# Softmax row sums in a transformer block: one running sum of four key tiles instead of a tree of pairs, with the diagonal's first tile in the last of them

## The chip, the core and the metric

The kernel runs on one core of a Trainium2 chip. The metric is the device time of one execution in microseconds (us). Before the change the median of three runs is 2449.43 us, with 2448.74 the lowest and 2451.66 the highest.

## The reference

One block of a conditioned transformer, all in float32: x is [2, 2048, 512], 16 heads of 32 dimensions, a hidden layer of 2048. The part that matters here is causal attention.

```
mod = silu(condition) @ Wada + bada            # six vectors per batch row
xm = layernorm(x) * (1 + sc_a) + sh_a
q, k, v = split(xm @ Wqkv)
scores = where(causal, q @ k.T * scale, -inf)
attn = softmax(scores);  out = attn @ v
x = x + gt_a * (out @ Wproj + bproj)
x = x + gt_m * (gelu(modulated layernorm(x) @ W1 + b1) @ W2 + b2)
```

The kernel never divides inside the attention loop. It computes the exponentials E of the scores less their row maximum, the product of E with v, and the row sums of E, and multiplies by the inverse sums afterwards.

## The kernel before

The program goes in stages: q, k, v of batch row 0; attention of row 0 (about 229 to 760 us in the profile); projection of row 0 and q, k, v of row 1; attention of row 1 (about 1085 to 1577 us); projection and the two layers of the hidden network. The change lies in the two attention stages, in `attention_phase`.

**Units and steps.** A stage has 16 units. A unit is a pair (c, i): c counts four groups of four heads (HC = 4), i counts four blocks of 512 queries (QB = 512). For c = 0 the blocks come in the order 0, 1, 2, 3, for the other groups in the order 0, 2, 1, 3. Unit 5, say, has i = 2, unit 14 has i = 1, and the last, unit 15, has i = 3. A unit goes through the key tiles of 128 keys (TQ = 4 to a query block) in steps. The 4i tiles ahead of the diagonal block take one step each. I write T for step 4i: it has the diagonal's first tile, with all 512 queries. Step T+1 has two narrower tiles (384 and 128 queries) side by side, and T+2 the last (256 queries).

**One step.** `scores_t` makes PSUM tiles `st`, one for each head: first a matmul of `fold` and `sel` that puts in minus the row maximum, then the product of keys and queries. The ScalarE (ACT) takes the exponentials, L576, into SBUF tiles `e`. On the diagonal steps the GpSimd (POOL) sets what lies above the diagonal to zero with an affine select, L582. Between these products PE also makes the scores `s` of coming units, whose row maxima the VectorE (DVE) reduces at L446 and L451; now and then such a score borrows a bank of `st`. The number per step comes from a plan of costs (`due`, `count`), in which the row sums don't appear. PE's matmuls are all issued at L199, and every engine works through its own list in the order in which it was written.

**Delayed work.** What uses the exponentials is put into a list, `pending`, with the number of the step at whose end it may be issued; `flush` issues what is due after the products of a step. The value products (`values`, tile `o`) of a step are issued two steps later (LAG = 2), so those of step T at the flush of T+2, those of T+1 at the flush of T+3, which is the first step of the next unit, and those of T+2 at the flush of T+4.

**Row sums.** They are matmuls with a block of ones (tile `sm`), a set of four for the four heads, the heads side by side on the PE array as for the value products. Ahead of the diagonal one set serves four tiles: POOL first adds tiles 0 and 1 (`pair_sums`, `ee<-e`), then 2 and 3, and then the two pairs in place (`four_sums`, `ee<-ee`), four adds each time, one for each head. The third addition is issued one step late (`later`); at the end of a unit it is split in two halves, one at step T after the selects of T, one at T+1 after those of T+1. Each diagonal step has sets of its own, issued with its value products. In the last unit of a stage the adds are DVE's (`add`, L604). Tiles `e` rotate through 12 buffers, tiles `ee` through 12.

Of the kernel before, what the change touches and what calls it, by code (L numbers as in the profile page):

```python
# [27 lines left out]
def dit_block_kernel(  # L28
# [32 lines left out]

    nc = tc.nc
    B, T, D = x.shape
    HID = W1.shape[1]
# [3 lines left out]
    HC = P // HD  # L70
    TQ = QB // P
# [1 line left out]
    MTT = MT // P  # L73
    NG = T // MT
    LAG = 2
    E_BUFS = 12
    EE_BUFS = 12
    AHEAD = 3

    const = ctx.enter_context(tc.tile_pool(name="const", bufs=1))  # L80
# [33 lines left out]
    for n in range(2):  # L114

        f = bp.tile([P, QB + P], F32R, tag=f"fold{n}", name=f"fold{n}")
# [84 lines left out]
    def act(ins):  # L201

        return tc.keep_in_program_order(ins)
# [322 lines left out]
    def attention_phase(row):  # L526
        b, vv, kst, qst = row.b, row.vv, row.kst, row.qst
        with pool(f"att{b}") as ap, pool(
# [6 lines left out]
            def scores_t(u, step, n):  # L535
# [29 lines left out]
                for h in range(HC):  # L565
                    at = 0
                    for j, q in tiles:
# [6 lines left out]
                        at += QB - q  # L574
                    e = ap.tile([P, QB], F32, tag="e", name="e", bufs=E_BUFS)
                    act(nc.scalar.activation(e[:, :w], sts[h][:, :w], AF.Exp))  # L576
# [19 lines left out]
            def new_sums():  # L596
                return [
                    ap.tile([P, QB], F32, tag="ee", name="ee", bufs=EE_BUFS)
                    for _ in range(HC)
                ]  # L600

            def add(u, h, dst, x, y):
                engine = nc.vector if u == len(units) - 1 else nc.gpsimd
                act(engine.tensor_tensor(dst, x, y, ALU.add))  # L604

            def pair_sums(u, es0, es1):
                out = new_sums()
                for h in range(HC):
                    add(u, h, out[h], es0[h], es1[h])
                return out  # L610

            def four_sums(u, ee0, ee1, heads):
                for h in heads:
                    add(u, h, ee0[h], ee0[h], ee1[h])

            def products(dst, lhs, es, q0, at, first, last):
                for h in range(HC):
                    mm(
                        dst[h * HD : (h + 1) * HD, q0:], lhs(h),
                        es[h][:, at : at + QB - q0], start=first, stop=last,  # L620
                    )

            def finish(u, o, sm):

                c, i = units[u]
                ot = ap.tile([P, QB], F32, tag="ot", name="ot", bufs=2)
                act(nc.scalar.copy(ot, o))
                sums = ap.tile([P, QB], F32, tag="sums", name="sums", bufs=2)
                act(nc.scalar.copy(sums, sm))
                nc.sync.dma_start(sums_d[b][u], sums[0:P:HD, :])  # L630
                nc.sync.dma_start(od[b][i][:, c, :], ot)


            pending = []
            now = 0

            def flush(upto):
                while pending and pending[0][0] <= upto:
                    pending.pop(0)[1]()
# [16 lines left out]
            def due(u, step):  # L656

                rate, past = 0.0, weight[step]
                for v in range(u + 1, len(units)):

                    left = sum(weight[step : max(step + 1, starts[v] - 3)])
                    rate = max(rate, (cum[v] - row.spent) / left)
                return row.spent + rate * past

            for u, (c, i) in enumerate(units):
                if NQ <= u + AHEAD < len(units):
                    row.load_queries(u + AHEAD)
                if u % NQ == 0 and c + 1 < C:
                    row.load_keys(c + 1, 0, NG)
                steps = len(steps_of[u])  # L670
                for n_step, tiles in enumerate(steps_of[u]):
                    last = n_step == steps - 1
                    if n_step == 0:
                        summed, later = set(), []
                        o = ps_op.tile([P, QB], F32, tag="o", name="o")
                        sm = ps_op.tile([P, QB], F32, tag="sm", name="sm")
                    ready = row.at

                    n = row.count(
                        due(u, starts[u] + n_step) - QB // 2, u + AHEAD - (n_step < 2)  # L680
                    )
                    es, rest = scores_t(u, n_step, n)
                    rest = len(row.todo) - rest
                    make_rows = False
                    if u + 1 < len(units) and row.rows_made == u + 1:
                        if last:
                            row.score(row.count(cum[-1], u + 1))
                        make_rows = last or (ready > u + 1 and n_step >= 1)
                    row.inverses(u, n_step)
                    if u == len(units) - 1:  # L690
                        row.prepare(n_step)
                    flush(now)
                    if make_rows:
                        row.rows(u + 1)
                    row.score(max(0, len(row.todo) - rest))

                    def tile_by_tile(dst, lhs, es, tiles, first, last):
                        at = 0
                        for n, (j, q) in enumerate(tiles):
                            products(  # L700
                                dst, lambda h: lhs(j, h), es, q, at,
                                first and n == 0, last and n == len(tiles) - 1,
                            )
                            at += QB - q

                    def values(es=es, tiles=tiles, c=c, o=o, first=n_step == 0, last=last):
                        tile_by_tile(
                            o,
                            lambda j, h: vv[:, j, (c * HC + h) * HD : (c * HC + h + 1) * HD],
                            es, tiles, first, last,  # L710
                        )

                    def row_sums(es, last, tiles=((0, 0),), sm=sm, summed=summed):
                        first = not summed
                        summed.add(len(summed))
                        tile_by_tile(sm, lambda j, h: ones[:, :HD], es, tiles, first, last)

                    if later:
                        four_sums(u, *later.pop(0))

                    pending.append((now + LAG, values))
                    if n_step >= i * TQ:
                        pending.append(
                            (
                                now + LAG,
                                lambda f=row_sums, es=es, tiles=tiles, last=last: f(
                                    es, last, tiles
                                ),
                            )
                        )  # L730
                    elif n_step % 2 == 0:
                        even = es
                    else:
                        ee = pair_sums(u, even, es)
                        if n_step % 4 == 1:
                            ee0 = ee
                        else:

                            end = n_step + 1 == i * TQ
                            for heads in ([(0, 1), (2, 3)] if end else [range(HC)]):  # L740
                                later.append((ee0, ee, heads))
                            pending.append(
                                (
                                    now + LAG + 2 + end,
                                    lambda f=row_sums, ee=ee0: f(ee, False),
                                )
                            )
                    if last:
                        pending.append((now + LAG, lambda u=u, o=o, sm=sm: finish(u, o, sm)))
                    pending.sort(key=lambda p: p[0])  # L750
                    now += 1
# [248 lines left out]
    with pool("wada") as wp, pool("qkv0") as qp, pool(  # L1000
# [110 lines left out]
        with pool("hl0") as hp:  # L1111
# [8 lines left out]
            quarters.store()  # L1120

    attention_phase(row)


    first, row = row, Row(1)
    with pool("qkv1") as qp, pool("ps_qkv1", bufs=6, space=PSUM) as ps_mm:
# [22 lines left out]
        with pool("hl1") as hp:  # L1149
# [5 lines left out]
            quarters.store()  # L1155

    attention_phase(row)
    ps_s_cm.__exit__(None, None, None)

# [4 lines left out]
    with ExitStack() as mlp:  # L1164
# [248 lines left out]
        for m in range(NM):  # L1413
            h = [
                [
                    mp.tile([P, 4, MT], F32, tag="h4", name="h4", bufs=2 * FC // 4)
                    for _ in range(FC // 4)
                ]
                for _ in range(2)
            ]  # L1420
# [87 lines left out]
```

## Time and profile before

| What | Value |
|---|---|
| median of the runs | 2449.43 us (2448.74 to 2451.66) |
| profiled execution, its own time | 2449.97 us |
| span of the profile | 2448.3 us |
| PE busy | 2409.8 us, 98% of the span |
| DVE busy | 1348.9 us, 55% |
| POOL busy | 986.8 us, 40% |
| ACT busy | 894.3 us, 37% |
| mean granted TensorE clock | 0.994 |

The span is from the first to the last instruction; the profiled execution's own time has 1.67 us around it. A busy share is an average over stages that differ, so it has to be read by stage. A group of instructions is given by its line, engine, operation and tiles (out<-in), its count, its busy time and the mean duration of one; matmuls overlap, so a matmul's price is read from the distance between starts. A matmul in float32 leaves two records. In the timeline a row has start, length, engine, line, operation and the number of merged instructions.

### The profile page before, as it was taken

How to read it: one execution, taken by the hardware profiler on the slowest of the kernel's cores; microseconds unless marked ns; L12 is line 12 of the kernel's file. 1: busy time of each engine (PE TensorE's matmuls, PEld its weight loads, DVE VectorE, ACT ScalarE, POOL GpSimd, SP SyncE). 2: the span in 40 equal slices, each digit the busy share in tenths (PEclk: the TensorE clock that was granted, in tenths of full speed). 3: DMA queues.
4: the chain of work that ended last, by engine and by line, in shares of the span. 5: the costliest groups of instructions: out<-in, count | busy, mean ns of one | idle time of the engine just before them, and what ended most of it. 6: DMA issues, size and time to landing. Idle time of an engine off the chain costs nothing. (4 is left out here: it accounts for less than half of the span.)

```text
span 2448.3 us, 31029 instructions
## 1 busy us (share of the span) xinstructions
PE 2409.8 (98%) x10989; PEld 1174.7 (48%) x10989; DVE 1348.9 (55%) x2828; ACT 894.3 (37%) x1668; POOL 986.8 (40%) x1167
## 2 busy tenths in 40 slices
PE   8999999999999999999999999999999999999998
PEld 3445555555554444555555555444444444444443
DVE  3455766666656636566666666673354263343424
ACT  2212555555554112255555555523213212312310
POOL 1051886776773460078677678312002101200200
PEclk9999999999999999999999999999999999999999
DMA  6667115151225795530515123362223223222322
GB/s 224 210 222 195 45 31 121 27 113 44 83 99 181 231 309 170 145 70 23 117 40 113 45 64 118 135 204 84 86 94 134 90 95 131 93 90 87 119 86 99
DMA packets 132853, 285.72 MB, mean 117 GB/s; under 512 B 13473, under 2 KB 42701, under 8 KB 127833
## 3 DMA queue, kind: packets, MB, share of 16 engines
q1 hardware_dynamic: 126224, 257.46, 35.4%
q0 software_dynamic: 6384, 26.25, 3.0%
q8 instruction: 86, 1.41, 0.2%
q14 instruction: 71, 0.57, 0.1%
q10 hardware_dynamic: 88, 0.02, 0.0%
HBM read 209.76 MB, written 81.79 MB: 119 GB/s over the span
## 5 line engine op out<-in xcount | busy, mean ns | idle before, releaser
L576 ACT ACTIVATE e<-st 128x512 f32<-128x512 f32 (+1 forms) x1152 | 574.1, 578 | 459.6 <-PE st L199 402.3
L451 DVE TENSOR_REDUCE mx<-s 128x1 f32<-128x512 f32 x606 | 408.7, 687 | 220.9 <-PE s L199 220.0
L604 POOL TENSOR_TENSOR ee<-e 128x512 f32<-128x512 f32 x336 | 421.1, 1298 | 210.1 <-ACT e L576 210.1
L199 PE MATMUL s<-kst,qst 128*128 128x512 f32 (+3 forms) x1032 | 465.3, 453 | 5.8 <-DVE mx L451 2.9
L199 PE MATMUL st<-qst,kst 128*128 128x512 f32 (+3 forms) x1280 | 411.3, 389 | 0.0
L446 DVE CUSTOM_DVE_ANT_0 junk<-s,causal 128x512 bf16<-128x512 f32 (+3 forms) x426 | 208.9, 490 | 156.3 <-PE s L199 148.3
L199 PE MATMUL o<-e,vv 128*32 128x512 f32 (+3 forms) x2560 | 293.6, 540 | 0.0
L1279 POOL TENSOR_TENSOR c<-c 128x512 f32<-128x512 f32 x32 | 40.8, 1275 | 625.6 <-DVE c L1241 606.0
L199 PE MATMUL ps_h<-sx,w 128*128 128x512 f32 x640 | 286.7, 592 | 0.0
L199 PE MATMUL ps_y<-sh,w 128*128 128x512 f32 x640 | 277.8, 594 | 0.0
L199 PEld LDWEIGHTS st<-qst,kst 128*128 128x128 f32 x1280 | 229.0, 189 | 94.5 <-issue 62.5
L199 PEld LDWEIGHTS s<-kst,qst 128*128 128x128 f32 x1032 | 195.0, 189 | 155.6 <-DVE mx L451 49.3
L199 PE MATMUL ps_qk<-xmT,wqkv 128*128 128x512 f32 x512 | 241.5, 600 | 2.2 <-DVE xmT L256 2.2
L582 POOL TENSOR_SCALAR_AFFINE_SELECT e<-e 128x128 f32<-128x128 f32 (+1 forms) x384 | 122.8, 353 | 268.7 <-ACT e L576 265.7
L1241 DVE TENSOR_TENSOR h<-c,ps_h 128x512 f32<-128x512 f32 x128 | 88.0, 687 | 232.5 <-PE ps_h L199 232.5
L604 POOL TENSOR_TENSOR ee<-ee 128x512 f32<-128x512 f32 x168 | 212.3, 1300 | 0.0
L199 PEld LDWEIGHTS ps_h<-sx,w 128*128 128x128 f32 x640 | 121.1, 190 | 150.2 <-issue 149.5
L199 PEld LDWEIGHTS ps_y<-sh,w 128*128 128x128 f32 x640 | 121.3, 191 | 148.5 <-issue 147.1
L1265 ACT ACTIVATE h<-h,cols 128x512 f32<-128x512 f32 x128 | 92.4, 722 | 181.6 <-DVE h L1241 181.6
L199 PE MATMUL st<-fold,sel 32*128 32x512 f32 (+1 forms) x1152 | 149.3, 482 | 2.1 <-DVE mhl L467 1.0
L199 PEld LDWEIGHTS ps_qk<-xmT,wqkv 128*128 128x128 f32 x512 | 94.9, 192 | 98.7 <-issue 92.6
L199 PEld LDWEIGHTS st<-fold,sel 32*128 32x128 f32 x1152 | 58.8, 182 | 147.6 <-ACT e L576 75.3
(128 smaller groups left out, 2359.0 us busy)
## 6 DMA issues: line engine op xcount, KB each, us to landing
qst<-q SPq DMA_DIRECT2D x128, 256.0 KB
w<-w1d SPq DMA_DIRECT2D x34, 896.0 KB
w<-w2d SPq DMA_DIRECT2D x28, 1024.0 KB
kst<-k SPq DMA_DIRECT2D x24, 1024.0 KB
q<-hl SPq DMA_DIRECT2D x32, 512.0 KB
k<-hl SPq DMA_DIRECT2D x32, 512.0 KB
kst<-k SPq DMA_DIRECT2D x32, 256.0 KB
w<-in_L_cond_W_dram POOLq DMA_DIRECT2D x64, 128.0 KB, 4.5
```

What stands on the lines that cost most here:

```text
L199: return tc.keep_in_program_order(nc.tensor.matmul(*args, **kw))
L446: nc.vector.tensor_tensor_reduce(junk[:, :w], s[:, :w], causal[:, QB - w :], 1.0, MASKED, ALU.add, ALU.max, m,)
L451: nc.vector.tensor_reduce(m, s[:, :w], axis=AX.X, op=ALU.max)
L576: act(nc.scalar.activation(e[:, :w], sts[h][:, :w], AF.Exp))
L582: nc.gpsimd.affine_select(d, d, pattern=[[0, len(tiles)], [1, P]], compare_op=ALU.is_ge, fill=0.0, base=0, channel_multiplier=-1,)
L604: act(engine.tensor_tensor(dst, x, y, ALU.add))
L1241: nc.vector.tensor_tensor(dst, x, y, op)
L1265: nc.scalar.activation(d, d, AF.Gelu, bias=col(r_b1 + chunk, 1))
L1279: nc.gpsimd.tensor_tensor(c1_, c1_, c2_, ALU.subtract)
```

## The change

`pair_sums`, `four_sums` and the list `later` go. In each group of four steps ahead of the diagonal, step 1 now begins a chain with the sum of tiles 0 and 1 (`begin_chain`), step 2 adds its tile to it and step 3 adds its own (`add_to`). The number of adds for four tiles stays at twelve. In units with i > 0 the last chain also takes the exponentials of step T, after that step's selects: four adds more, and no set of row sums for T alone. The chain that takes T is summed at the flush of T+4, and the sums of step T+1 move from the flush of T+3 to that of T+4, after the chain's. Units with i = 0 have no chain and keep their sums. There are 16 buffers for `e`, so four steps, and 8 for `ee`.

```
-    E_BUFS = 12
-    EE_BUFS = 12
+    E_BUFS = 16
+    EE_BUFS = 8
...
-            def pair_sums(u, es0, es1):
-                out = new_sums()
+            def add_to(u, chain, es):
                 for h in range(HC):
-                    add(u, h, out[h], es0[h], es1[h])
-                return out
-
-            def four_sums(u, ee0, ee1, heads):
-                for h in heads:
-                    add(u, h, ee0[h], ee0[h], ee1[h])
+                    add(u, h, chain[h], chain[h], es[h])
+
+            def begin_chain(u, es0, es1):
+                chain = new_sums()
+                for h in range(HC):
+                    add(u, h, chain[h], es0[h], es1[h])
+                return chain
...
-                    if later:
-                        four_sums(u, *later.pop(0))
-
                     pending.append((now + LAG, values))
-                    if n_step >= i * TQ:
+                    sums_of, wait = None, 0
+                    if n_step < i * TQ:
+                        k = n_step % TQ
+                        if k == 0:
+                            even = es
+                        elif k == 1:
+                            chain = begin_chain(u, even, es)
+                        else:
+                            add_to(u, chain, es)
+                        if k == TQ - 1 and n_step + 1 < i * TQ:
+                            sums_of, wait = (chain, False), 2
+                    elif i and n_step == i * TQ:
+                        add_to(u, chain, es)
+                        sums_of, wait = (chain, False), 2
+                    else:
+
+                        sums_of, wait = (es, last, tiles), i > 0 and not last
+                    if sums_of:
                         pending.append(
-                            (
-                                now + LAG,
-                                lambda f=row_sums, es=es, tiles=tiles, last=last: f(
-                                    es, last, tiles
-                                ),
-                            )
+                            (now + LAG + wait, lambda f=row_sums, s=sums_of: f(*s))
                         )
-                    elif n_step % 2 == 0:
-                        even = es
-                    else:
-                        ee = pair_sums(u, even, es)
-                        if n_step % 4 == 1:
-                            ee0 = ee
-                        else:
-
-                            end = n_step + 1 == i * TQ
-                            for heads in ([(0, 1), (2, 3)] if end else [range(HC)]):
-                                later.append((ee0, ee, heads))
-                            pending.append(
-                                (
-                                    now + LAG + 2 + end,
-                                    lambda f=row_sums, ee=ee0: f(ee, False),
-                                )
-                            )
```

More of the change, by code (lines that the diff above doesn't have):

```diff
@@ L673, in attention_phase @@
                     if n_step == 0:
-                        summed, later = set(), []
+                        summed = set()
                         o = ps_op.tile([P, QB], F32, tag="o", name="o")
```

## The prediction

> **What bounds the kernel now.** I read the page first, then the busy time by stage, the groups by form, and the timelines of PE, POOL and ACT around the ends of two units. The two attention stages are the only ones that the change touches.
>
> ```profile
> PE 2409.8 (98%) x10989; PEld 1174.7 (48%) x10989; DVE 1348.9 (55%) x2828; ACT 894.3 (37%) x1668; POOL 986.8 (40%) x1167
> ```
> ```profile
> 229.00:760.00 531.00, 528.81 (x3613) 271.74 (x3613) 351.68 (x845) 293.73 (x586) 367.16 (x428) 0.99 0.30 76
> ...
> 1100.00:1580.00 480.00, 478.16 (x3314) 243.42 (x3314) 316.16 (x759) 265.99 (x532) 333.19 (x394) 1.00 0.29 76
> ```
> ```profile
> L604 POOL TENSOR_TENSOR ee<-e 128x512 f32<-128x512 f32 x336 | 421.1, 1298 | 210.1 <-ACT e L576 210.1
> ...
> L604 POOL TENSOR_TENSOR ee<-ee 128x512 f32<-128x512 f32 x168 | 212.3, 1300 | 0.0
> ...
> L199 PE MATMUL sm<-ee,ones 128*32 128x512 f32 x384 | 51.1, 604 | 0.0
> ```
> In the second block the columns are the stretch, its length, and busy time of PE, PEld, DVE, ACT, POOL. PE is busy 528.8 of 531.0 us in the first attention stage and 478.2 of 480.0 in most of the second: whatever PE no longer does there is gained, as long as it still waits for nothing. POOL is the next fullest, 367 of 531 (69%), and it is far from evenly filled: it idles in the units of i = 0 and works without a gap at the ends of the others. The list of waits has PE and its weight loads waiting for POOL hardly at all (5.5 us in 17 pieces of at most 0.4), so today's margins hold. The question is whether they hold after the change.
>
> **What leaves PE.** The end of unit 5 (i = 2), PE's timeline:
>
> ```profile
> 415.49 1.07 PE L199 MATMUL o<-e,vv 128*32 128x512 f32 x8
> 416.49 0.49 PE L199 MATMUL s<-kst,qst 128*128 128x512 f32 x1
> ...
> 418.48 1.07 PE L199 MATMUL o<-e,vv 128*32 128x512 f32 x8
> 419.36 1.04 PE L199 MATMUL sm<-e,ones 128*32 128x512 f32 x8
> 420.33 0.50 PE L199 MATMUL st<-fold,sel 32*128 32x512 f32 x4
> ...
> 422.70 1.07 PE L199 MATMUL o<-e,vv 128*32 128x384 f32 x16
> ```
> A set of four value products alone takes 415.49 to 416.49, 1.00 us; followed by a set of row sums 418.48 to 420.33, 1.85. Four row sums so cost 0.85 us, start to start (the durations overlap and add up to more). The change drops the row sums of the first diagonal tile in every unit of i > 0: 12 units a batch row, 24 in all, 96 matmuls of two profile records each, which the instruction lists of the two builds confirm. 24 x 0.85 = **20.4 us off PE**. The sums of tiles T+1 and T+3 are only moved one flush later, into a run of the same kind of matmul: no set more or less, no new change between kinds, so I put this at nothing. Scores on PE, exponentials and DMA issues keep their order; at each stage's end two neighbouring stores swap, which costs nothing as the first load that needs them, r<-sum, follows both either way, and twice a stage a reduction of DVE (0.69 us) swaps with small neighbours, in stretches where PE waited for DVE under 0.5 us: nothing too.
>
> **What goes to POOL.** Outside the last unit of each row, 22 units get four adds more (88). In the trace eight adds stretch from 401.58 to the next start at 411.52: 1.24 us each, 4.97 for a set of four, 109 us in all. It lies beside PE, but in a worse place. Before, a group of four steps gave POOL four adds at its step 1, four at step 3, four at the next step 0 (split in two halves around the selects at a unit's end). Now steps 1, 2, 3 give four each, and step T four more. The adds of T stand in POOL's queue ahead of the selects of step T+1, and PE's value products wait for those selects. That is the new wait. Its neighbour, the chain's own sum, is not wanted before two flushes later.
>
> I walk POOL's queue for two units, with times of exponentials from ACT's timeline, 4.97 us for four adds and 1.01, 1.45 and 1.05 us for the selects of T, T+1, T+2 (from start-to-start).
>
> ```profile
> 401.58 10.01 POOL L604 TENSOR_TENSOR ee<-e 128x512 f32<-128x512 f32 x8
> 411.52 1.07 POOL L582 TENSOR_SCALAR_AFFINE_SELECT e<-e 128x128 f32<-128x128 f32 x4
> 412.55 2.55 POOL L604 TENSOR_TENSOR ee<-ee 128x512 f32<-128x512 f32 x2
> 415.03 1.50 POOL L582 TENSOR_SCALAR_AFFINE_SELECT e<-e 128x256 f32<-128x256 f32 x4
> ```
> ```profile
> 711.73 2.06 ACT L576 ACTIVATE e<-st 128x512 f32<-128x512 f32 x4 [0.18 <-PE st L199]
> 715.15 2.06 ACT L576 ACTIVATE e<-st 128x512 f32<-128x512 f32 x4 [1.36 <-PE st L199]
> 718.95 2.06 ACT L576 ACTIVATE e<-st 128x512 f32<-128x512 f32 x4 [1.73 <-PE st L199]
> 722.09 2.07 ACT L576 ACTIVATE e<-st 128x512 f32<-128x512 f32 x4 [1.08 <-PE st L199]
> ```
> ```profile
> 728.61 1.07 PE L199 MATMUL o<-e,vv 128*32 128x384 f32 x16
> ```
> Unit 5: the adds begin at 384.46 as they do now, and run in one piece: sets end at 389.4, 394.4, 399.4; second chain 404.4, 409.3, 414.3 (its last exponentials were ready at 407.5). Selects of T 415.3, adds of T 420.3, selects of T+1 421.7, of T+2 422.8. PE wants T at 418.48 (3.2 us to spare) and T+1 at 422.70 less the 0.85 saved, 421.85: **0.1 us to spare**. Before, those selects were done at 416.5.
> Unit 14 (i = 1, scores run out, so steps last 3.4 us and not 3.7): chain begins at 708.17, sets end at 713.1, 718.1, 723.1; selects of T 724.1; adds of T 729.1; selects of T+1 from 729.1 to 730.5. PE wants them at 728.61 - 0.85 = 727.76: the first head's is 1.7 us late, the last 2.7.
> The same walk over the other nine units of i > 0 and POOL sums in the first stage gives waits of 0.1 to 0.7 us in three of them and 0.2 to 1.2 to spare in the rest; with unit 14 some 3.5 us a stage. Behind that wait on PE stands everything: the next scores, so ACT and DVE too. **Two stages: 7 us lost.**
>
> **A smaller loss** is in the score banks. After the flush of T+2 PE starts the next step's max products, into banks that ACT (exponentials) and DVE (one borrowed bank) must have read. In unit 5 DVE's last read of a borrowed bank ends at 419.38 and ACT's at 419.13; PE would now come at 418.48 + 1.00 = 419.48, just after. Read so for each unit, DVE is late by 0.1 to 0.2 us in five of a stage's twelve: 1 us a stage, **2 us in all**.
>
> DVE's eight adds more (four in each row's last unit, 0.62 us each by spacing) end about 4 us before PE asks for that chain (T's exponentials are done at 765.8, PE's closing run of sums reaches the chain near 771), and the two products for the projection that they push back are wanted only past 773; with that cover gone they would cost 2.5 us a stage. Buffers: exponentials 12 to 16, sums 12 to 8, equal space. The 6.5 us that ACT waits for POOL to free exponentials may vanish; ACT idles 43% of the stage and PE did not wait for it, so nothing.
>
> **Two rules of the Trainium skill** bear on this. The page's rows give a POOL add 1298 ns, the spacing 1.24 us. "Perfetto Trace Analysis", section "GPSIMD Engine Instruction", calls a GPSIMD span in the profile unreliable and says to time by spacing. I follow it, and it matters: with 1.298 in the walk, some 28 adds on average since POOL last idled make each select of T+1 1.5 us later, and the sum turns to a loss (below). The other speaks against the change: "SBUF — State Buffer", section "Who interferes with whom", has a DVE instruction with two SBUF inputs and a reading GpSimd instruction exclude each other. DVE's score reductions take at most one input from SBUF; only the last unit's DVE adds meet it, beside POOL's selects. By the rule four selects could each wait out an add, 2.5 us a stage, 5 in all. In the trace, adds beside those selects keep their pace (two in 1.38 us at 763.91), so I take 0 and keep 5 for the range.
>
> **Sum:** -20.4 + 7 + 2 = -11.4 us against the profiled execution's 2449.97 (span 2448.3 and 1.67 around it): **2438.5 us**. The median of the runs, 2449.43, is 0.5 below the profiled time, inside what this sum can tell.
>
> **Rivals.** *Full gain* (0.14): the selects come just in time, for each wait of PE also pushes back what it needs next, so that a lateness isn't paid twice. For it: six of those nine units have time to spare. -20.4, 2429.5.
> *Swallowed* (0.15): PE gets to the flushes of T+2 and T+3 0.85 us earlier and waits there for banks or selects in most units. For it: spare times of 0.1 us. Against it: the walked mean is 0.4 us a unit. If a unit loses 0.85 the whole is 0: 2449, the range of this case 2445 to 2454.
> *POOL becomes the bound* (0.08), the slower side: the price of an add. At 20.4/22, a mean wait of 0.93 us a unit, nothing is left; as 0.4 is there already and about 28 adds stand ahead, 0.02 to 0.04 us an add, 2 to 3%, decides. At 1.298 us, waits come to about 1.2 us, 26 in all: 2457. Against it: the spacing is 1.24 in every set that I read, whether fresh or in place (`ee<-ee` 4.96 a set), and an in-place add follows its forerunner by four instructions in both versions.
> *The change doesn't do what it says*: excluded by the instruction lists for PE and POOL.
>
> **How the numbers follow.** The forecast's own case (0.63) runs from 2433 to 2444.5. Measurement can tell about 0.2%, 4.9 us. Faster is forecast and full gain, 0.77; same 0.15; slower 0.08. The range runs from full gain to well into the swallowed case, 2429 to 2447.
>
> **What would show it.** Right: PE busy some 20 us less, `sm` on `e` of 128x512 from 256 matmul records to about 64; POOL busy about 110 us more; value products of 128x384 waiting for POOL `e` selects, 5 to 9 us over both stages, longest in units 14; stage lengths 5 to 6 us less each. Wrong: selects late in every unit by a microsecond (POOL's spacing above 1.28), or `st` waiting for DVE or ACT by half a microsecond a unit, or no wait at all and 20 us gained.

## The result and the profile after

| | before | after |
|---|---|---|
| median of 5 runs each | 2449.58 us (2448.74 to 2451.66) | 2438.84 us (2437.49 to 2440.26) |
| ratio, 95% interval | | 0.9955 (0.9941 to 0.997) |
| profiled execution, span | 2449.97, 2448.3 us | 2439.56, 2437.9 us |
| first attention stage, first `fold` product to first `ps_o` | 549.22 us | 542.95 us |
| second attention stage, the same | 548.32 us | 543.96 us |
| between the two stages | 254.28 us | 258.43 us |

The change makes the kernel 10.7 us faster; the interval of the ratio is 7.3 to 14.4 us. The stages gain 6.3 and 4.4 us in the profile, and 4.15 of that go again between them. The line of the page and the groups by form that answer to those of before:

```profile
PE 2394.4 (98%) x10797; PEld 1172.4 (48%) x10797; DVE 1349.5 (55%) x2836; ACT 893.7 (37%) x1668; POOL 1091.5 (45%) x1255
```
```profile
L605 POOL TENSOR_TENSOR ee<-ee,e 128x512 f32<-128x512 f32 x424 | 528.8, 1285 | 4.8 <-ACT e L577 4.5
L200 PEld LDWEIGHTS o<-e,vv 128*32 128x32 f32 x2560 | 60.4, 108 | 97.5 <-issue 79.9 <-POOL e L583 11.1 <-PE st L200 2.6
L200 PE MATMUL o<-e,vv 128*32 128x384 f32 x256 | 30.5, 497 | 2.0 <-POOL e L583 2.0
L200 PE MATMUL sm<-e,ones 128*32 128x512 f32 x64 | 9.7, 684 | 0.0
```
The last three of these groups before the change:
```profile
L199 PEld LDWEIGHTS o<-e,vv 128*32 128x32 f32 x2560 | 58.9, 108 | 108.4 <-issue 96.8 <-POOL e L582 5.5 <-PE st L199 2.6
L199 PE MATMUL o<-e,vv 128*32 128x384 f32 x256 | 27.2, 497 | 0.0
L199 PE MATMUL sm<-e,ones 128*32 128x512 f32 x256 | 33.9, 601 | 0.0
```

PE has 192 records fewer, which are those of `sm` on `e` at 128x512, 256 before and 64 now. POOL has 88 instructions more and 104.7 us more of busy time. PE's busy time fell by 15.4 us and not by 20, and the third of the groups says where a part of the rest is: the value products of step T+1 (128x384) were busy for 27.2 us with no wait before. They now take 30.5 us and wait another 2.0 us for POOL's selects, 5.3 us in all. A wait between two heads of one set hides in the busy time of such a row, since the record of the matmul before it lasts on (497 ns in the mean). The idle time alone, 2.0 us, would show less than half of the loss.

The end of unit 5, where the prediction left 0.1 us to spare, in POOL's and PE's timelines of the changed kernel:

```profile
399.10 9.98 POOL L605 TENSOR_TENSOR ee<-ee,e 128x512 f32<-128x512 f32 x8
409.01 1.06 POOL L583 TENSOR_SCALAR_AFFINE_SELECT e<-e 128x128 f32<-128x128 f32 x4
410.03 5.01 POOL L605 TENSOR_TENSOR ee<-ee,e 128x512 f32<-128x512 f32 x4
414.97 2.50 POOL L583 TENSOR_SCALAR_AFFINE_SELECT e<-e 128x256 f32<-128x256 f32 x8
```
```profile
416.58 1.07 PE L200 MATMUL o<-e,vv 128*32 128x384 f32 x16
```

The third line is the new work, four adds of T. Of the eight selects in the fourth, the first four are those of T+1; they end 0.10 us before PE starts at 416.58. Nothing waits. In unit 14 it is otherwise:

```profile
712.13 1.04 POOL L583 TENSOR_SCALAR_AFFINE_SELECT e<-e 128x128 f32<-128x128 f32 x4
713.15 4.99 POOL L605 TENSOR_TENSOR ee<-ee,e 128x512 f32<-128x512 f32 x4
718.09 2.48 POOL L583 TENSOR_SCALAR_AFFINE_SELECT e<-e 128x256 f32<-128x256 f32 x8
```
```profile
718.55 2.13 PE L200 MATMUL o<-e,vv 128*32 128x384 f32 x16 [1.01 <-POOL e L583]
720.61 0.50 PE L200 MATMUL st<-fold,sel 32*128 32x512 f32 x4
```

The adds end at 718.09, then the selects come head by head. PE waits 1.0 us for the first head and is then held up inside the set: it lasts from 718.55 to the next start at 720.61, 2.06 us where unit 5 takes 1.00. So this one place costs 2.1 us. The same reading for each unit of i > 0 in the first stage, from the end of the last select of T+1 to PE's start of the set: 0.01 to 0.7 us to spare in units 1, 2, 3, 5, 7, 9 and 11, 1.8 and 1.4 in units 6 and 10, and late in units 13 (0.56) and 14. The second stage shows the same within 0.3 us. Before, the spare time of these units was 2.9 us in unit 14 and 5.5 to 6.6 in the others.

The loss between the stages has a line too. PE's timeline of before, and then of after, where the first scores of row 1 are computed among the products for its queries and keys:

```profile
888.89 0.44 PE L199 MATMUL s<-kst,qst 128*128 128x384 f32 x1 [0.90 <-DVE mx L446]
```
```profile
881.61 0.44 PE L200 MATMUL s<-kst,qst 128*128 128x384 f32 x1 [3.39 <-DVE mx L447]
```
And what DVE did in the meantime, in its timeline of after:
```profile
875.90 0.69 DVE L809 SCALAR_TENSOR_TENSOR hl<-ps_qk,hl 128x512 fp32r<-128x512 f32 x1 [1.08 <-ACT hl L808]
879.85 0.69 DVE L212 BATCH_NORM_STATS2 stat<-x 128x6 f32<-128x512 f32 x1 [3.26 <-DMA x<-in_x_dram]
...
881.26 0.28 DVE L447 CUSTOM_DVE_ANT_0 junk<-s,causal 128x128 bf16<-128x128 f32 x1
```

DVE's row maximum at 881.26, which PE needs, stands in DVE's queue behind a statistic that waits for a load of x. From 834 to 884 us the DMA engines are 97% busy. PE arrives 10 us earlier than before and stands still 2.5 us longer there.

### The profile page after: what moved, and what is told of

It is laid out like the page before. It is cut to its first block, busy times and chain, and to the rows that moved or that the text cites. A ratio compares the mean times of both kernels' runs of the same rounds, so it can differ in the third digit from the quotient of the medians.

```text
span 2437.9 us, 31025 instructions
## 1 busy us (share of the span) xinstructions
PE 2394.4 (98%) x10797; PEld 1172.4 (48%) x10797; DVE 1349.5 (55%) x2836; ACT 893.7 (37%) x1668; POOL 1091.5 (45%) x1255
## 4 chain that ended last, share of the span: by engine, by line
PE 94%; DVE 2%; DMA 2%; POOL 1%; issue 1%; ACT 0%; DVEq 0%; SPq 0%; ACTq 0%; POOLq 0%
PE st L200 20%; PE ps_y L200 16%; PE ps_h L200 16%; PE o L200 11%; PE s L200 10%; PE ps_qk L200 9%; PE ps_o L200 4%; PE sm L200 4%; PE ps_v L200 4%; DMA k<-hl 1%; PE ps_xt L208 1%; POOL ee L605 1%; PE ps_o L208 0%; DVE junk L447 0%; DMA x<-in_x_dram 0%
## 5 line engine op out<-in xcount | busy, mean ns | idle before, releaser
L605 POOL TENSOR_TENSOR ee<-ee,e 128x512 f32<-128x512 f32 x424 | 528.8, 1285 | 4.8 <-ACT e L577 4.5
L605 POOL TENSOR_TENSOR ee<-e 128x512 f32<-128x512 f32 x168 | 210.3, 1284 | 105.6 <-ACT e L577 105.3
L583 POOL TENSOR_SCALAR_AFFINE_SELECT e<-e 128x128 f32<-128x128 f32 (+1 forms) x384 | 119.7, 347 | 255.8 <-ACT e L577 253.0
```

The costliest lines, as they stand in the source:

```text
L583: nc.gpsimd.affine_select(d, d, pattern=[[0, len(tiles)], [1, P]], compare_op=ALU.is_ge, fill=0.0, base=0, channel_multiplier=-1,)
```

## The experiments

Edits are against the changed kernel, where nothing else is said. Three comparisons were made after that of the result, each with runs of the kernel before on the same chip (median 2448.36 us in the first, 2449.91 in the second, 2450.52 in the third). To compare traces step by step, I took the start of the first exponential in each step of each unit, less that of the stage's first; where two kernels drift apart is where one of them waits.

**1. The adds of T moved behind the selects of T+1.** In all units but each row's last one, the four adds are issued one step later:

```
                     elif i and n_step == i * TQ:
-                        add_to(u, chain, es)
+                        held = es
+                        if u == len(units) - 1:
+                            add_to(u, chain, es)
...
                     else:
+                        if i and n_step == i * TQ + 1 and u < len(units) - 1:
+                            add_to(u, chain, held)
```

> The changed kernel, with the four adds of tile T issued one step later on POOL (after the selects of T+1, not ahead of them), in all units but the last of each stage. Work on every engine is the same. Theory (what the change loses is the wait of the T+1 value products for selects behind the adds, 2.1 us in each unit 14, plus about 1 us a stage of bank waits that stay): no wait of o on POOL selects in unit 14 any more, 4 us less than the changed kernel, about 2434.5 to 2435, ratio to the kernel before 0.994. Rival (the shortfall against 20.4 us has another cause, the score banks or the TensorE clock): same time as the changed kernel, 2438.8, ratio 0.9955.

Measured: 2431.53 us, ratio 0.9924 (0.991 to 0.9937). Unit 14 in the timelines of POOL and PE, and the group of the value products' weight loads:

```profile
712.20 2.48 POOL L583 TENSOR_SCALAR_AFFINE_SELECT e<-e 128x128 f32<-128x128 f32 x8
714.65 4.99 POOL L605 TENSOR_TENSOR ee<-ee,e 128x512 f32<-128x512 f32 x4
```
```profile
717.58 1.07 PE L200 MATMUL o<-e,vv 128*32 128x384 f32 x16
718.58 0.50 PE L200 MATMUL st<-fold,sel 32*128 32x512 f32 x4
```
```profile
L200 PEld LDWEIGHTS o<-e,vv 128*32 128x32 f32 x2560 | 59.0, 108 | 93.6 <-issue 80.1 <-POOL e L583 5.5 <-PE st L200 2.6
```

The same eight selects and four adds, the other way round: PE finds the selects done 2.9 us before it asks, and the weight loads' wait for POOL is back from 11.1 to the 5.5 us of before. Step by step this kernel equals the changed one within 0.2 us up to unit 13 of the first stage. Then it gains 0.6 us where unit 13's products of T+1 are made and 2.1 where those of unit 14 are. In the second stage the gains are 0.4 and 2.1. The selects of T+1 cost the changed kernel 2.7 and 2.4 us in the two stages, **5.1 us in all, all of it in two units**. The medians lie 7.3 us apart, where 4 were expected, but they are of two comparisons and contain what the clock and the wait between the stages did in each.

**2. The same once more**, with the edit of experiment 1, beside the changed kernel without an edit.

> The deferred adds once more, beside the changed kernel. Theory (two waits of 2.1 us are gone and two stages start at like clocks): 4 us below after_again, ratio to it 0.998, to the kernel before 0.992 to 0.994. Rival (the 7 us between them in the first comparison were chips and clocks): within 2 us of after_again.

> The changed kernel once more, on the chip of the runs beside it, as their measure. Every theory: 2438 to 2440 where the kernel before is at 2449, ratio 0.9945 to 0.9965.

Measured: 2435.27 us, ratio 0.9933 (0.992 to 0.9946) for the first, 2437.0 us, ratio 0.9943 (0.9929 to 0.9957) for the changed kernel. The steps part in the same two units by the same amounts (0.6 and 2.1, 0.4 and 2.1). The medians, though, are only 1.7 us apart and the means 2.7, where 4 were expected; by the medians alone the rival, within 2 us, would have it. The two profiles show what covers the difference: with the adds deferred the granted clock was at half for 10.2 us at the start of the second stage and for 3.4 us between the stages, in the changed kernel for 6.8 us and not at all. Over both comparisons, ten runs each, the means are 2432.2 and 2437.5 us, with standard errors of 0.9 and 0.7: 5.3 us apart, near the 5.1 of the steps; only half of these runs were made side by side. Single medians of this kernel moved by nearly 4 us between the comparisons, so five runs alone would not have shown this.

**3. T left out of the sums.** Neither POOL (DVE in the last unit) nor PE sums T, so the row sums lack it:

```
                     elif i and n_step == i * TQ:
-                        add_to(u, chain, es)
                         sums_of, wait = (chain, False), 2
```

> The changed kernel without any sum of tile T: the chain has the group's four tiles only, and T's exponentials are left out of the row sums (this part of the computation is missing). PE has the same list as the changed kernel, POOL 88 adds less and DVE 8 less. It gives PE's gain without POOL's price. Theory: 20.4 us less 2 us of bank waits, about 2431.5 to 2435 (no wait for selects), the same as e1_defer within 1 us. Rival that POOL's 88 adds cost time by themselves (109 us of work beside PE, sharing memory or semaphores): well below e1_defer, by 3 us or more. Rival that the banks take back more than was read: no better than the changed kernel, 2438.8.

Measured: 2432.12 us, ratio 0.9932 (0.992 to 0.9945). Apart from the first steps of each stage, which the last section explains, its steps are those of experiment 1 within 0.1 us in the first stage, and within some 0.5 in the second. So the 88 adds cost nothing in the first stage where they don't stand ahead of the selects, and no more than those 0.5 us in the second. It also gives the price of the 24 sets, since its clock at the stages' starts was that of before (0.86 granted from 218 to 242 us, 0.88 from 1018 to 1046): its stages last 539.27 and 539.15 us, 9.95 and 9.17 us less than before, 19.1 in all.

**4. The chain alone.** T and T+1 keep their own sums at their old places; only the form of the additions is new. The last chain's sums come at the flush of T+3.

```
-                        if k == TQ - 1 and n_step + 1 < i * TQ:
+                        if k == TQ - 1:
                             sums_of, wait = (chain, False), 2
-                    elif i and n_step == i * TQ:
-                        add_to(u, chain, es)
-                        sums_of, wait = (chain, False), 2
                     else:
-                        sums_of, wait = (es, last, tiles), i > 0 and not last
+                        sums_of, wait = (es, last, tiles), 0
```

> The chain and the new buffers, but tile T keeps its own row sums on PE at its old place, and T+1 too: the order of the adds alone is changed. Theory: POOL finishes the adds of the last group earlier or as early as before and nothing is queued between the diagonal's selects, so the kernel before within 0.1%, 2448 to 2451. Rival (the chain form itself costs, since steps 1, 2 and 3 of a group now bring 15 us of adds in three steps of 3.5 us): selects of T late, 2452 or more. Rival (16 buffers for exponentials take away ACT's 6.5 us of waits and this shows): 2444 or less.

Measured: 2453.2 us over 21 runs, ratio 1.0022 (1.0015 to 1.0028). This was missed; it should have been no different from before. The list of PE's waits from 229 to 760 us has one line more than that of before:

```profile
PE s L200 <- DVE fold L512: 0.6, 2, 0.3
```

The two places are in units 4 and 8, where the last work of units 3 and 7 is done. My edit had moved a set of row sums: before, the last chain's set came at the flush of T+4, now at that of T+3, so the second and third step of the next unit follow 0.85 us closer on one another. I took it that DVE then has 0.85 us less to finish `fold` for the scores that come; the next experiment's traces show something else.

**5. The moved set put back**, beside the kernel of experiment 4 once more; the edit is against that kernel:

```
-                            sums_of, wait = (chain, False), 2
+                            sums_of, wait = (chain, False), 2 + (n_step + 1 == i * TQ)
```

> The chain-only kernel with the one set that it had moved put back: the last chain's row sums are issued at the flush of T+4, as before the change, and no longer at that of T+3. If the moved set made the chain-only kernel slower (DVE had 0.85 us less to finish the row maxima that the next score products wait for), the half-microsecond waits for DVE at units 4 and 8 are gone, and the time is that of before: 2448 to 2451, 0.9 to 2 us less span than the chain-only kernel. If the chain's form itself costs something (adds on POOL at steps 2 and 3 in place of steps 3 and 4), the waits stay or come elsewhere, and the time is 2452 to 2455.

> The chain-only kernel once more, beside the one with the set put back. If the moved set is its whole price, 1.5 to 2 us over that one, with the two waits a stage for DVE; the rest of its earlier 3.4 us more span then came from the clock at the stages' starts. If the chain's form costs, the two are alike.

Measured: 2452.36 us over 21 runs, ratio 1.0008 (1.0001 to 1.0015), with the set back; 2453.41 over 20 runs, ratio 1.0013 (1.0006 to 1.002), without. PE's timeline at the end of unit 3's work, first without, then with the set back:

```profile
376.26 0.38 PE L200 MATMUL st<-qst,kst 128*128 128x256 f32 x1
376.93 0.50 PE L200 MATMUL s<-kst,qst 128*128 128x512 f32 x1 [0.29 <-DVE fold L512]
```
```profile
374.11 0.39 PE L200 MATMUL st<-qst,kst 128*128 128x256 f32 x1
374.33 0.39 PE L200 MATMUL s<-kst,qst 128*128 128x512 f32 x1
```

The distance of the two starts is 0.67 us in the one and 0.22 in the other. DVE's timeline at the same place, in the same order:

```profile
376.05 0.83 DVE L512 TENSOR_TENSOR fold<-ps_m,tmask 128x640 fp32r<-128x640 f32 x1 [0.20 <-PE ps_m L208]
376.79 0.18 DVE L466 TENSOR_REDUCE s<-mx 128x16 f32<-128x32 f32 x1
```
```profile
372.88 0.20 DVE L466 TENSOR_REDUCE s<-mx 128x16 f32<-128x32 f32 x1
373.90 0.82 DVE L512 TENSOR_TENSOR fold<-ps_m,tmask 128x640 fp32r<-128x640 f32 x1 [0.53 <-PE ps_m L208]
```

With the set moved, `fold` stands ahead of the three short instructions that finish a unit's row maxima (L466 to L468); with the set put back, and before the change, it stands behind them. That is the only difference between DVE's lists of the two kernels. It occurs at four places, in units 4 and 8 of both stages, and the four waits are at these. Where `fold` is ahead, PE's score starts as it ends, at 376.9; where it is behind, the score starts at 374.33 and `fold` ends at 374.72. DVE was not short of time here, for it stood idle just before `fold` in both. The edit doesn't touch these instructions and the program's text has them in one order, so an engine's list can depart from the text; what turned them round is not known. By the steps the four places cost 0.35 to 0.42 us each, 1.6 us. The medians are 1.05 us apart, where 1.5 to 2 were expected. With the set back, no step of the first stage from unit 1 on moves against before by more than 0.2 us, so the chain as such costs nothing there. The time is 0.2 to 3.7 us above that of before all the same, above the 2451 that I had allowed and by the number in the stretch of the rival (the form itself costs, 2452 to 2455), whose waits are not there. Its profile shows a lower clock at the stages' starts (0.79 and 0.82 granted, before 0.86 and 0.88), which gives 2.1 us by the steps, and in the second stage 0.9 us in shifts of 0.2 to 0.3 us. One profile can't say whether that holds for 21 runs: this remainder stays open.

**6. A dose.** One more add of 128x512 on POOL, of no use to the output, behind the adds of T in 22 units, ahead of the selects of T+1:

```
+            spare = ap.tile([P, QB], F32, tag="spare", name="spare")
...
                         add_to(u, chain, es)
+                        if u < len(units) - 1:
+                            act(nc.gpsimd.tensor_tensor(spare, es[0], es[1], ALU.add))
```

> The changed kernel with one more POOL add of 128x512 after the four of tile T, into a tile that nobody reads, in every unit that has a chain but the last of each stage (22 adds of 1.24 us, 27 us of POOL work). Theory (the selects of T+1 are within 0.1 to 0.8 us of being late in most units): each unit's selects come 1.24 us later, and taking off the spare time read in the changed kernel's trace PE waits some 9 us more a stage: 2455 to 2458, slower than the kernel before. Rival (only unit 14 is near the edge, other waits are absorbed): 2 x 1.24 us more, 2441.

Measured: 2458.67 us, ratio 1.0037 (1.0025 to 1.005), 0.7 us above the stretch that was expected. The groups of the value products and of the added instructions, and then unit 14 on POOL and PE:

```profile
L200 PE MATMUL o<-e,vv 128*32 128x384 f32 x256 | 45.6, 511 | 5.9 <-POOL e L583 5.6
...
L735 POOL TENSOR_TENSOR spare<-e 128x512 f32<-128x512 f32 x22 | 28.9, 1311 | 0.0
```
```profile
722.86 5.00 POOL L605 TENSOR_TENSOR ee<-ee,e 128x512 f32<-128x512 f32 x4
727.80 1.28 POOL L735 TENSOR_TENSOR spare<-e 128x512 f32<-128x512 f32 x1
729.01 2.50 POOL L583 TENSOR_SCALAR_AFFINE_SELECT e<-e 128x256 f32<-128x256 f32 x8
```
```profile
729.49 2.99 PE L200 MATMUL o<-e,vv 128*32 128x384 f32 x16 [2.19 <-POOL e L583]
732.41 0.80 PE L200 MATMUL st<-fold,sel 32*128 32x512 f32 x4
```

One add more in front of the selects (727.80 to 729.01 here, 1.21 us) makes nine of eleven units late in the first stage. The products of T+1 now take 45.6 us and wait 5.9 more, against 30.5 and 2.0: 19.0 us more, close to the difference of the medians (2458.67 less 2438.84, 19.8, of two comparisons). 22 adds at 1.24 us are 27.3 us of POOL's time, and PE loses 70% of it. Not all of that is waiting: by the steps the two units 14 lose 2.4 and 2.7 us more than in the changed kernel, about twice an add, since right behind PE's wait the clock is at half for 3.4 us (0.50 granted from 730 to 733 us). The kernel is now slower than before.

**7. T kept out of the chain in unit 14 alone**, with a set of its own at the flush of T+4:

```
-                        add_to(u, chain, es)
+                        if u == len(units) - 2:
+                            pending.append(
+                                (now + LAG + 2, lambda f=row_sums, s=(es, False, tiles): f(*s))
+                            )
+                        else:
+                            add_to(u, chain, es)
```

> The changed kernel, with tile T of unit 14 alone kept out of the chain and summed by PE as a set of its own (at the flush of T+4): two sets of 0.85 us more on PE, eight adds less on POOL. Theory (unit 14 is the only one where the selects cost PE more than a few tenths, 2.1 us there): 2 x (2.1 - 0.85) = 2.5 us below after_again. Rival (the waits are spread over all units): 1.7 us above it or, with a lesser wait gone, equal.

Measured: 2434.52 us, ratio 0.9937 (0.9925 to 0.995). Against the changed kernel beside it, the steps differ by no more than 0.3 us up to unit 14 and by 1.2 us in each stage after it. It saves the wait of 2.1 us and pays the set of 0.85, which makes the two prices that the prediction set against each other visible in one unit.

**8. The deferred adds with the dose of experiment 6**, the idle add behind them; the edit is against the kernel of experiment 1, with the same tile `spare`:

```
                         if i and n_step == i * TQ + 1 and u < len(units) - 1:
                             add_to(u, chain, held)
+                            act(nc.gpsimd.tensor_tensor(spare, held[0], held[1], ALU.add))
```

> The deferred version with the same idle POOL add as in e4_dose (22 of 1.24 us), right behind the deferred adds of T, so behind the selects of T+1. Theory (the place in POOL's queue costs, not the work): equal to e1_again within 1 us, although the same add cost some 20 us in e4_dose. Rival (POOL's total work is at its limit, so any add is paid): 9 us or more above e1_again.

Measured: 2432.74 us, ratio 0.993 (0.9918 to 0.9942). It was expected within 1 us of the kernel without the dose. It is 2.5 us below that kernel's runs beside it and 1.2 above its earlier ones, which differ by 3.7 between them. The stages say more, for they last 540.51 and 541.15 us with the dose, and without it 540.34 and 541.04 in one profile and 539.45 and 541.52 in the other. The dose is there, and PE's products of T+1 don't see it (27.3 us and no wait, by form):

```profile
L740 POOL TENSOR_TENSOR spare<-e 128x512 f32<-128x512 f32 x22 | 28.5, 1293 | 0.0
L200 PE MATMUL o<-e,vv 128*32 128x384 f32 x256 | 27.3, 497 | 0.0
```

The same 22 adds cost 20 us ahead of the selects and nothing that could be measured behind them. For these adds the place in the queue decides, not POOL's load.

## Why the prediction came out

**The sets that left PE** (-20.4): right. Experiment 3 has 19.1 us less in the two stages at the clock of before; with the 1.0 us for the banks, below, that makes 20.1.

**POOL's queue** (+7): right in mechanism and place, a little too large. Unit 5 was walked to 0.1 us to spare and had 0.10. Unit 14 was to be late by 1.7 us for the first head and 2.7 for the last; PE waited 1.0 and lost 2.1. Three more units were to lose 0.1 to 0.7 each; only unit 13 did, 0.5. The cost is 5.1 us in place of 7. Of the difference, the step that failed is one that was costed at nothing: the row sums of T+1, moved from the flush of T+3 to that of T+4. PE's timelines around the start of unit 14's chain, first of before, where POOL begins the chain at 708.17, then of after, where it begins at 697.09:

```profile
704.60 1.07 PE L199 MATMUL o<-e,vv 128*32 128x384 f32 x16
705.49 1.05 PE L199 MATMUL sm<-e,ones 128*32 128x384 f32 x16
```
```profile
697.74 1.06 PE L200 MATMUL sm<-ee,ones 128*32 128x512 f32 x8
698.62 1.05 PE L200 MATMUL sm<-e,ones 128*32 128x384 f32 x16
```

The set of unit 13's T+1 lay ahead of the chain's start and now lies behind it. In a unit with i = 1 everything up to the selects of T+1 happens in these few steps, so PE asks for them 0.88 us later, counted from the chain's start, than the walk had it. 2.7 us less 0.88 is 1.8; PE lost 2.1. The rest of the difference is the three units of 0.1 to 0.7, of which only unit 13 came late.

**The banks** (+2): right in kind, half the size. By starts, PE comes 0.10 to 0.16 us late to the next scores in five units of the first stage (1, 3, 7, 9 and 13), as predicted in number; but in unit 2 a wait of before became 0.3 us shorter. That is 0.5 us; in the second stage this last gain is missing and it is 0.7, so about 1 in all. Five times 0.1 to 0.2 us had been rounded up to 1 us a stage.

**What was costed at nothing.** In the last unit DVE's adds end before 758.7 and PE reads that chain at 761.77, 3.1 us later, where the prediction had 4; the two products that follow were not waited for. ACT's wait for POOL to free exponentials did not vanish: in the list of waits it grew from 6.5 us to 20.2, 10.9 of them behind the selects and 9.3 behind the adds. ACT's idle time (45% of the stage by the prediction's own block, not 43%) was no bound, so it still costs nothing.

**The two rules of the Trainium skill.** A POOL add of 128x512 has 1285 ns in the row and 1.24 us from start to start (eight in 9.91 us at 399.10). Experiment 6 confirms the choice: its extra add takes 1.28 us in its row, and the selects start 1.21 us after it. With 1.298 us in the walk the kernel would have come out slower, and it did not. The exclusion of a DVE instruction with two SBUF inputs and a reading POOL instruction ("SBUF — State Buffer", "Who interferes with whom") was taken as 0 and not as 5 us. As a price that held; as a reason, "adds beside those selects keep their pace" saw only one side. The last unit of the first stage, DVE's timeline, and then the view of POOL's instructions at L583 from 755 to 762 us (shortest, median and longest in ns):

```profile
755.73 0.69 DVE L605 TENSOR_TENSOR ee<-ee,e 128x512 f32<-128x512 f32 x1 [0.21 <-POOL e L583]
756.60 2.06 DVE L605 TENSOR_TENSOR ee<-ee,e 128x512 f32<-128x512 f32 x3 [0.18 <-POOL e L583]
758.58 1.69 DVE L427 TENSOR_TENSOR kst<-kst,qst 128x512 f32<-128x512 f32 x2
```
```profile
L583 POOL TENSOR_SCALAR_AFFINE_SELECT e<-e x12: 286/347/852, 755.4 to 761.6; 128x128 f32<-128x128 f32 x8, 128x256 f32<-128x256 f32 x4
```

DVE's adds lose little: three last 1.98 us, 0.66 each, where adds with an idle POOL take 0.60 (four in 2.41 us from 749.41). But the selects lose much: of the four of T+1, three run beside the last add and the two products, take 0.85 us each and start 0.80 us apart; the fourth runs after them and takes 0.40. They are done at 760.90, and PE's products of T+1 start at 760.90. Before, PE had 1.5 us to spare there. This agrees with the rule; the loss fell on POOL, and it used up the margin to the last 0.1 us without yet costing time: from PE's products of T to the chain's sums it is 1.75 us, as in experiment 3, where DVE has no such adds. By this margin one more DVE instruction there would be paid for; that was not tried.

**The step that the prediction did not have.** It let the first stage's gain pass unchanged to the second. Between them PE waits for DVE, and DVE for a load, 0.90 us before and 3.39 in the profile after. In seven traces of the faster kernels that wait is 1.4 to 3.7 us, in the five others 0.9 to 2.2. So some of the gain is given back there, about 1 us in the mean; with such scatter the size isn't settled, and no run tried that wait by itself.

**The sum once more.** In the stages the changed kernel gains 20.4 less 5.1 less 1.0, 14.3 us. Its profile has 10.6 (6.27 and 4.36): 2.3 more were lost to the clock, 0.7 and 1.6 us at the two starts, and about 1.2 in small shifts of the second stage. Then 2.5 us went to the wait for DVE between the stages and 1.7 to the clock there (half from 882.7 to 886.1 us, right behind that wait), while the time up to the first stage was 3.5 us shorter, which has nothing to do with the change (it scatters over 4 us in all twelve traces). The medians give 10.7 and 12.9 us in the two comparisons. The predicted 11.4 was so near partly because two terms taken too large, 3 us together, stood in for a wait and a clock that the sum did not contain.

**The rivals.** The full gain was not reached, but experiments 1 and 3 show that the order of POOL's queue is most of what kept it back; deferring the adds beats both kernels. That PE would meet waits in most units is excluded by the spare times. The slower rival was the true danger: its mechanism is what experiment 6 switches on, with one add's time a unit.

## What to carry to other kernels

Moving work to an engine that is 40% busy isn't judged by that share but by what stands behind the moved work in its queue, and how long until someone wants it. Walk the queue with start-to-start times, unit by unit, and look for the shortest unit: the loss sits in one or two places, not in the mean. What isn't urgent goes behind what is: the adds were wanted two flushes later, the selects at once, and swapping the two was worth 5 us for nothing.

## What the hardware showed besides

At the start of each attention stage the granted TensorE clock falls to half for 6.8 us in some executions and 10.2 us in others, in all twelve traces. The stretch from 218 to 242 us of before, of after and of experiment 3; the column behind POOL's is the granted clock:

```profile
218.00:242.00 24.00, 22.99 (x115) 11.90 (x113) 10.81 (x23) 10.68 (x20) 3.96 (x12) 0.86 0.84 195
```
```profile
218.00:242.00 24.00, 22.99 (x121) 12.72 (x123) 9.90 (x22) 11.46 (x22) 5.10 (x13) 0.79 0.90 196
```
```profile
218.00:242.00 24.00, 22.99 (x114) 12.12 (x114) 10.54 (x23) 10.56 (x20) 3.96 (x12) 0.86 0.88 202
```
And, in shorter stretches of after, the same place and the one behind the wait between the stages:
```profile
226.00:230.00 4.00, 4.00 (x17) 3.21 (x16) 0.82 (x1) 2.58 (x5) 1.63 (x4) 0.50 0.98 199
...
883.00:885.00 2.00, 2.00 (x4) 0.82 (x3) 0.44 (x1) 0.00 (x0) 0.85 (x2) 0.50 0.97 367
```

PE counts as busy while the clock is at half, so only the clock column tells of it. If PE had matmuls to do all the time, 10.2 us at half clock would lose 5.1 us and 6.8 us would lose 3.4. By the steps the longer stretch at a stage's start costs 0.6 to 1.6 us more than the shorter, and where it lies counts too: in experiment 4's second stage one of 6.8 us costs 0.7 us more than that of before. This is of the size of the differences that these experiments have to tell apart. The Trainium skill, "TensorE: Matmul & The Clock Gate", in its Part 1, has a gate with a half and a full rate and a free-running window of about 3.4 us. The lengths of 6.8 and 10.2 us, two and three such windows, agree with it, and a free-running window would explain that the length varies. It puts the fall to half down to a window in which PE is idle; here PE's last gap before it is the 1.0 us at the stage's first `fold`. The traces have other falls that do follow a gap: between the stages, at the end of four of the five longest waits for DVE (2.3 to 3.7 us) or within 1.2 us after it, and at none of the other seven (0.9 to 2.2), and in experiment 6 behind the waits of 2.2 us in both units 14. Most of these gaps are shorter than the page's window. What sets the clock down was not tried, so that stays open.
